# Transposing quantised FFN rows in float32r: DMA copies of thirteen batches into float32r tiles, with the remaining order of steps written anew

## The chip, the cores and the metric

The kernel runs on one core of a Trainium2 chip. The engines are named as in the profile: PE is the matrix engine (PEld its weight loads), DVE the vector engine, ACT the scalar engine, POOL the general engine, SP the engine that issues most DMAs. The metric is the time on the device of one execution, in microseconds, of which a smaller one is better. Times are given as the median of several runs; the profile is of one further execution.

## The reference

One transformer layer over `x` of 16 batches, 256 rows and 256 columns, in float32. What matters here is its last part, a gated FFN whose inputs and weights are quantised in blocks of 16 along the last axis:

```python
def fp4_quant_dequant(x):
    xb = x.reshape(shape[:-1] + (shape[-1] // BLOCK, BLOCK))
    scale = jnp.max(jnp.abs(xb), axis=-1, keepdims=True) / 6.0
    scale = jnp.maximum(scale, jnp.float32(1e-12))
    xn = xb / scale
    idx = jnp.searchsorted(_MID, jnp.abs(xn))
    q = _GRID[idx] * jnp.sign(xn) * scale
    return q.reshape(shape)
...
gate = fp4_linear(x, w_gate)
y = fp4_linear(x, w_up)
h = jax.nn.silu(gate) * y
return fp4_linear(h, w_down)
...
x = x + _L0_attn_ref(_L0_cond_ref(x, mask_SxS_bk1, cond_256, ...), ...)
x = x + _L0_ffn_ref(_L0_cond2_ref(x, cond_256, ...), ...)
```

`fp4_linear` quantises both operands and multiplies. The hidden size is 704. Ahead of the FFN stand an attention with 16 heads and a modulated norm, a recurrence over the rows (RWKV), and a spectral rotation by quaternions.

## The kernel before

The work of each batch is cut into stages, each a Python generator that yields after a few instructions. A stage and a batch make a name of two characters: `a` asks (loads x, projects q, k and v), `t` attends, `l` leaves the attention (output projection and norm), `m` mixes (the recurrence), `r` rotates and quantises the FFN's input, `h` and `i` make the hidden rows of the first and second 128 rows of the batch (`hidden`), `d` and `e` transpose them (`turn_h`), `f` multiplies by the down weights (`down`). The batch is a hex digit. `W` and `V` are the weights of the FFN, prepared once by `in_weights` and `out_weights`.

The order of all instructions is written out by hand in `ORDER` (L28), 1884 names; each occurrence runs its generator up to the next `yield`, and within the block at L1113 every engine executes its instructions in just that order. `BANKS` (L83) gives for each of 749 PSUM tiles, in order of allocation, which of the eight banks it takes. An engine that waits holds up everything behind it in its own queue, SP included: it issues the loads of x (L165), the spreads of q and k by way of DRAM (L704 and L708, one store and eight loads each) and the stores of the output (L1091, L1064), in the order of the steps.

The hidden rows go this way, for each batch and 128 rows, in two chunks of 384 and 320 columns: PE computes gate and up in PSUM (L1003); ACT takes the tanh (L1015); DVE forms the product (L1017, L1019); `quant_bank` quantises it with DVE (L554 to L557), ACT (L559), DVE again (L561, L562), and last POOL multiplies by the block scales into the SBUF tile `hq` (L564). `hq` has four buffers. `turn_h` (L1026) then has PE transpose the 704 columns of `hq` in six blocks of up to 128, three to a PSUM tile, in `turn_part` (L604, the transposes at L608), and ACT copies the result to `hT` (L1033 to L1037), from which `down` reads (L1072, L1079, and L1052 for the last batches). `turn_part` also serves the down weights in `out_weights`. `late(b)` (L662) is true for the last three batches, which take some other paths in `rotate` and `down`.

All of this is float32, and so are `ident` (L200), the identity matrix of the transposes, and `hq`. The one use of float32r, a type of four bytes for PE, is the attention's scores (L771), whose `qT` and `kT` tiles are of that type and are filled by DMA, with the source seen as float32.

Of the kernel before, what the change touches and what calls it, by code (L numbers as in the profile page):

```python
# [8 lines left out]
F32 = mybir.dt.float32  # L9
BF16 = mybir.dt.bfloat16  # L10
F32R = mybir.dt.float32r
# [7 lines left out]
P = 128  # L19
# [13 lines left out]
m0 m0 m0 a2 l1 a2 m0 l1 t2 W5 V0 R t2 t2 t2 a3 m0 V1 m0 m0 t2 t2 m0 W3 l1 t2 W3 m0 l1 m0 t2 t2 t2 t2 R t2 t2 t2  # L33
R m0 V0 t2 W0 W0 l1 m1 a3 W4 a3 a3 m0 V0 W3 l1 t2 m1 W3 a3 t2 t2 W2 W2 W0 A m1 m1 l2 A m1 m1 W4 l2 r0 m1 l2 m1
l2 r0 a4 a3 m1 m1 l2 l2 m1 m1 l2 m2 m1 m1 l2 m1 a3 m2 t3 a3 t3 m2 t3 t3 t3 m1 a4 t3 r0 r0 t3 r0 t3 a4 t3 t3 t3
m2 a4 t3 t3 a5 m2 W2 a4 V1 m2 t3 a4 t3 r0 t3 m2 m1 r0 t3 r0 a4 r1 m2 m2 a4 r1 t3 r1 r0 a4 W2 a5 a4 l3 l3 a6 m2
l3 V1 r1 m2 r0 a5 i0 a5 m2 i0 r1 r1 m2 i0 l3 V1 a4 t4 r1 m2 t4 t4 h0 i0 V1 t4 t4 i0 V1 m2 a5 t4 i0 h0 i0 h0 h0
t4 t4 i0 V1 t4 t4 t4 t4 i0 t4 a5 l3 t4 a5 r1 l3 r1 t4 m2 m2 h0 l3 a5 m3 l3 m3 t4 V1 a5 m3 i0 i0 a5 r2 r1 t4 h0
t4 m3 m3 r2 i0 m3 h0 a5 m3 l4 l4 a6 m3 l4 m3 m3 i0 a6 a5 l4 m3 m3 V1 a6 m3 t5 m3 t5 i1 i0 m3 t5 t5 i0 m3 t5 t5
e0 h0 i1 i1 e0 a6 t5 i1 t5 t5 t5 t5 h0 t5 t5 m3 i1 l4 t5 r2 a6 r2 t5 r2 l4 a7 t5 l4 i1 i1 d0 h0 i1 a6 h0 m4 r3  # L40
l4 m4 m4 h0 a6 a6 t5 d0 h1 m4 h0 r3 r2 i1 t5 h1 h1 a6 a6 i1 h1 m4 m4 h0 a7 r2 h1 i0 i1 h0 a6 h1 m4 a7 m4 a7 i1
m4 t6 h1 e0 t6 m4 m4 e0 t6 m4 l5 t6 i1 l5 t6 t6 r2 h0 d0 l5 m4 i1 h1 i1 t6 r2 m4 a7 m4 t6 d0 t6 l5 l5 t6 t6 r3
t6 t6 r3 t6 l5 a7 r2 e1 l5 r3 m4 a7 t6 d1 r3 i2 a7 r3 a7 f0 i1 i2 h2 i2 r3 i2 r3 f0 m5 l5 h2 e1 m4 a7 m5 a8 i2
h2 m5 h2 a7 i2 i2 h2 h1 r4 h2 h1 a7 h2 h1 d1 f0 h1 t7 i2 f0 t6 t7 f0 r4 t7 t7 h1 e1 t7 h1 m5 t7 t6 e1 t7 m5 h1
a8 t6 t7 m5 t7 t7 t7 a8 r4 h1 m5 t7 h2 d1 a8 r4 t7 d1 m5 r4 a8 a8 d2 l6 t7 m5 l6 l6 l6 i2 m5 i2 i2 r4 r3 m5 a8
i2 m5 r4 a8 l6 m5 h2 t7 a8 m5 h2 i2 h2 a8 m5 f1 l6 i2 m5 i2 i3 a9 a8 h2 h2 l6 i3 f0 f1 i3 h2 f1 i3 a8 l6 h2 m6
h2 d2 m6 m6 t8 f1 t8 t8 t7 t8 e2 i2 f1 i3 m5 t8 d2 r5 i3 i3 d2 r5 t7 a9 t7 t8 t8 t8 e2 t8 i3 e2 t8 a9 t8 a9 t8
t8 e3 m6 l7 m6 t8 l7 m6 t8 a9 r4 h3 h3 l7 l7 a9 r4 m6 m6 a9 l7 h3 e2 m6 a9 h3 l7 h3 a9 m6 m6 h3 f2 l7 i3 a9 i3
m6 i3 m6 h3 f2 i3 l7 m7 h3 m6 i3 i3 m6 m6 a9 aa m7 h3 i3 h3 h3 f1 h3 f2 m7 a9 e3 t9 t8 t9 t9 t9 f2 m6 r4 d3 f2
i3 t9 r6 h3 h3 t9 d3 e3 t8 h3 r6 t8 t9 h3 aa t9 t9 d3 e3 r5 r5 t9 r5 aa i4 i4 t9 l8 d3 t9 i4 m7 i4 aa i4 ab r5  # L50
h4 l8 i4 r5 m7 l8 h4 i4 f2 l8 aa t9 h4 h4 aa t9 m7 r5 h4 h4 l8 l8 i4 m7 h4 l8 t9 m7 m7 aa aa h4 m7 m7 i4 m7 m7
d4 m8 i4 i4 f3 aa aa l8 m7 m8 h4 m7 i4 i4 f3 m7 h4 m7 i4 m8 aa d4 r7 f3 h4 aa h4 i4 h4 ta f3 ta ta t9 f3 ta r7
ab h4 ac h4 ta e4 r7 t9 ab r7 e4 ta ab i4 ta r7 h4 r5 t9 ta ta r7 m8 ta ta ta ta r7 d4 r5 r6 ab r6 ta m8 m8 e4
m8 ab ab ta r6 m8 m8 m8 m8 l9 ab r6 h5 l9 m8 i5 h5 r6 i5 d4 m8 ab h5 l9 i5 h5 ab i5 e4 h5 i5 h5 h5 h5 ab l9 i5
m8 m8 r6 h5 h5 h5 tb h5 tb ta tb i5 tb m8 m8 r6 ab h5 l9 f4 tb l9 tb tb h5 i5 h5 tb e5 f4 ta ta e5 tb h5 tb tb
tb l9 f4 d5 r8 f4 f4 l9 tb r8 d5 r6 d5 ac m9 f4 tb r7 r8 r7 la tb la h6 h6 la r8 r8 h6 i5 i5 h6 m9 la d5 h6 la
i5 r7 i5 m9 m9 la ac m9 r8 m9 i5 m9 m9 ac i5 m9 la m9 ma m9 ac i6 m9 i7 m9 ac r8 h6 r8 ac m9 i5 i5 m9 i6 i6 ac
e5 m9 ac i7 h6 ac la i7 h6 ma e5 i6 f5 i7 f5 i6 i7 ma i6 i7 m9 f5 ad i6 f5 d6 h7 r9 h6 i6 i7 h6 h6 h6 ac f5 h7
h7 ac d6 tc tc r9 h6 tb h6 h7 tc ad tc ad ae h7 tc tc h6 tb h7 tc ad h7 tc tc tb r9 tc ad tc tc i7 ma h7 tc r9
h6 d6 ad i6 r9 ma tc e6 ma ad tc i6 i6 ma i6 h7 r9 r9 i7 f5 ma i6 r8 ma ad e6 r8 i6 lb ad h7 i7 h7 i6 h8 ma i6  # L60
i7 ma ad i7 ma e6 ma h7 h8 d6 i7 lb ad r9 e6 i7 h8 ma h7 ma r9 lb h7 i7 h8 td lb tc h7 ad td h8 td td td ma h8
lb h8 td e7 lb lb f6 lb f6 e7 mb td f6 i7 mb tc mb h8 ma tc h7 td td d7 f6 ra d7 i8 td f6 td i8 td ra r9 td e7
ae i8 i8 td d7 ra i8 mb i8 e7 f6 ra i8 i9 ae d7 i9 mb ra mb i9 i9 lc ra mb ae mb td h8 mb lc ae h8 i9 lc i8 i9
lc ra ae i9 lc mb h8 ae lc h8 mb h9 lc ra h8 mc ae h8 h9 h9 ra ae mb h9 ae h8 mb mb td d8 lc i8 h9 i8 mb h9 mc
mb f7 ra f7 h8 i8 mb i8 h9 f7 td d8 mc f7 te i8 f7 te rb rb ae te te td e8 i8 rb te te mc h9 i8 mc mc ae rb e8
af f3 rb ld ld rb i9 mc mc mc te ld rb mc te ld te mc mc te te ld mc te i8 te mc mc te mc te d8 af te e8 ld af
te e9 ld md h9 i9 h9 ld h9 te md md md af i9 af d8 mc af i9 md h9 md C rb i9 rb h9 af ha af md i9 e8 i9 md md h9
ha ha md ha f8 md ia ia ha af ia md md ia ha af h9 ia f8 md md i9 f8 ia ia af tf e9 rb tf f8 rc tf tf ia d9 tf
f8 ha tf ia md tf rc tf d9 tf rc i9 ha ia ia tf ia tf tf rc tf tf ia ea e9 e9 ib da rc tf h9 tf d9 ib ib f7 ia
ia le rc rc ib tf f8 le hb ib d9 hb rc tf hb ib le ha le hb le ha ib f9 rc le f9 md le hb ha hb da me ia ha le  # L70
hb ib ha f9 f9 ha ea ha rc ea me ea f9 eb me me me rd ha ib da hb ib me ib me db rd ib rd me rd lf me ib hb da
lf hb ib lf rd rd lf hb lf ib me rd me rd hb lf me hb me lf lf me rd rd ib fa fa hb me db mf eb hb eb hb fa me
db mf mf hc ic hc hc db me fa hc mf re ic fa ic hc ic re hc hc eb re mf ic re ic mf hc re re mf f9 fb re dc hc
fb hc re ic hc dc mf hc mf mf hc re mf mf hc ic ec hc fb mf ic ec ic hc hd ic mf dc mf re id ic ie mf hd ic dc
mf id fb id ic ic id ic hd rf hd id ec ec fc fb id ie rf rf ie id id fb rf fc hd rf ed id hd ed id id hd fc id
hd rf hd rf dd hd id rf ie dd hd he rf id hd he rf id id hd he ed hd he if ie ed hd hd ie if ie ie ie ie ie ie
dd dd he if if ie he he he fa fd ee he fd fd de ee if he ie he if he hf ie fd ie hf he if de he hf if ee he if
ee if ef if hf he hf de de hf fe if fe hf hf hf if hf hf if hf df hf if if fe ef hf hf C fc fe ff df ef ef hf fd
df df C fc fe C ff fc ff ff ff ff ff
"""  # L80


BANKS = """  # L83
0123456702 1345670521 3470521364 7320516473 0275164237 5164023571 6043175415 3752406175 2406137541 6035741604
3165042763 1504276315 0246701245 6012465307 2164375023 4756234571 0254371254 3172130671 2507136254 7163204617
3246172530 2615304527 0615627045 6207341502 6731502617 0341635042 3570143527 6013756021 3750425405 6130253607
4163075165 3210746251 0736251063 2416521425 7045273645 0273165407 3416523071 4530276135 2074630146 5370462715
3064537106 2536713460 2153470134 6702346753 6154321675 3421673245 7054763473 1052674273 1520731207 3561403256
1743256412 3054167401 5274301574 3065120373 4561207356 3074305126 4732065704 3215431275 0312670435 1274531604
7531045261 0675105402 5137205146 7250136247 5013473506 2435264053 7415602417 2516427460 3561207314 5017264210  # L90
7640327125 3020425264 6026516106 4106452410 156014205
"""


# [1 line left out]
def kernel(  # L96
# [28 lines left out]
    nc = tc.nc  # L125
# [4 lines left out]
    FF = w_gate.shape[0]  # L130
# [6 lines left out]
    const = ctx.enter_context(tc.tile_pool(name="const", bufs=1))  # L137
# [4 lines left out]
    wk = ctx.enter_context(tc.tile_pool(name="work", bufs=1))  # L142
# [5 lines left out]
    def bank(name):  # L148
        at = next(plan, None)
        if at is None:  # L150
            spare[0] = (spare[0] + 1) % 7
            at = 7 if name == "pss" else spare[0]
        return psum.tile([P, 512], F32, tag=f"bank{at}", name=name)

    def ps():
        return bank("ps")
# [42 lines left out]
    nc.scalar.activation(early, mhalf, AF.Exp)  # L199
    ident = const.tile([P, P], F32, tag="ident", name="ident")  # L200
    make_identity(nc, ident)


    blank = const.tile([P, P], F32, tag="blank", name="blank")
# [398 lines left out]

    def turn_part(src, k0):  # L604
        pt = ps()
        for k in range(k0, k0 + 3):
            n = min(P, FF - k * P)
            nc.tensor.transpose(pt[0:n, (k - k0) * P : (k - k0 + 1) * P], src[:, k * P : k * P + n], ident)  # L608
        return pt[:, 0 : 3 * P].rearrange("p (k t) -> p k t", t=P)

    def out_weights(t):
# [50 lines left out]
    late = lambda b: b >= B - 3  # L662

    xTs, qks, oTs, xns, ys, x1s, xqs, hqs = {}, {}, {}, {}, {}, {}, {}, {}
# [330 lines left out]
    def hidden(b, tt):  # L995
        xqT = xqs[b]
        hq = None
        for f0, n in ((0, 384), (384, FF - 384)):
# [20 lines left out]
            nc.vector.scalar_tensor_tensor(h[:, 0:n], th, 0.5, h[:, 0:n], ALU.mult, ALU.mult)  # L1019
            if f0 == 0:  # L1020
                hq = wk.tile([P, FF], F32, tag="hq", name="hq", bufs=4)
                hqs[b, tt] = hq
            yield from quant_bank(h, n, hq[:, f0 : f0 + n])


    def turn_h(b, tt):  # L1026
        hq = hqs.pop((b, tt))
# [234 lines left out]
```

## Time and profile before

| | |
|---|---|
| median of 3 runs | 645.34 us (645.21 to 646.45) |
| the profiled execution | 645.53 us, of which span 643.7 |
| granted PE clock | 1.000 |
| DMA | 57.72 MB, mean 90 GB/s |
| DVE L936, reciprocal of 128x512 | 16 x 3343 ns |
| ACT L781, exponentials of the scores | 256 x 609 ns |

The span is the time from the first to the last instruction; the rest of the execution's time lies around it. A row of the profile names a line and engine, what is written and read, the count, the busy time and the mean length of one, and the idle time before it with what ended it. For PE, busy time is the union of overlapping instructions: the mean length of a matmul is its latency, and the distance from start to start of two that follow each other is what it takes of the engine. A float32 matmul stands as two records, a transpose as one. Over the span in 40 slices, PE, DVE and the DMA engines are busy as follows, in tenths:

```profile
PE   9999999999999999999999999999999999999996
...
DVE  7897899889898877999998999999999999999994
...
DMA  6643525334251425333420334203204100001001
```

### The profile page before, as it was taken

The page shows a single profiled execution, that of the slowest core. Times are in us where ns is not written, and L with a number is a line of the kernel's source. Part 1 is how long each engine was busy: PE and PEld are TensorE (multiplying, and loading weights), DVE is VectorE, ACT ScalarE, POOL GpSimd, SP SyncE. Part 2 cuts the span into 40 slices and gives each one's busy share as a digit, 9 for nine tenths or more (in the row PEclk, how much of TensorE's full clock was granted, in tenths as well). Part 3 has the DMA queues.
Part 4 walks back from the last instruction along what each step waited for, and adds up shares of the span by engine and source line. Part 5 has one row for each costly group of instructions (what it writes and reads, how often), then busy time and mean ns, then how long its engine had stood idle before and what let it go on. Part 6 is the DMA issues. An engine that isn't in the chain of part 4 may idle for free.

```text
span 643.7 us, 11304 instructions
## 1 busy us (share of the span) xinstructions
PE 635.6 (99%) x3936; PEld 475.9 (74%) x3936; DVE 579.0 (90%) x1178; ACT 391.2 (61%) x903; POOL 161.4 (25%) x214
## 2 busy tenths in 40 slices
PE   9999999999999999999999999999999999999996
PEld 7568877677777778777777777777877778776675
DVE  7897899889898877999998999999999999999994
ACT  3879784776757577674766546666483755433332
POOL 3353213222231122131221313113130122112220
PEclk9999999999999999999999999999999999999999
DMA  6643525334251425333420334203204100001001
GB/s 169 172 149 120 167 87 174 99 99 133 82 166 35 154 57 166 78 100 116 148 67 18 126 102 149 67 17 131 82 34 151 47 2 16 1 1 35 0 26 46
DMA packets 62848, 57.72 MB, mean 90 GB/s; under 512 B 36912, under 2 KB 40896, under 8 KB 62784
## 3 DMA queue, kind: packets, MB, share of 16 engines
q1 hardware_dynamic: 62416, 56.65, 29.4%
q8 instruction: 33, 0.54, 0.4%
q10 hardware_dynamic: 368, 0.28, 0.1%
q14 instruction: 31, 0.25, 0.1%
HBM read 38.03 MB, written 18.87 MB: 88 GB/s over the span
## 4 chain that ended last, share of the span: by engine, by line
PE 83%; DVE 12%; issue 2%; ACT 1%; DVEq 0%; ACTq 0%
PE ps L632 24%; PE ps L1003 18%; PE ps L793 9%; PE ps L644 8%; PE ps L1072 7%; PE pss L771 5%; PE ps L608 3%; PE ps L965 2%; PE pss L763 2%; DVE v L562 1%; DVE ps L554 1%; PE ps L656 1%; DVE ps L561 1%; DVE ps L1019 1%; PE ps L1079 1%
## 5 line engine op out<-in xcount | busy, mean ns | idle before, releaser
L1003 PE MATMUL ps<-guT,xqT 128*128 128x320 f32 (+1 forms) x512 | 165.6, 461 | 0.6 <-DVE v L562 0.6
L781 ACT ACTIVATE w<-pss 128x512 f32<-128x512 f32 x256 | 133.6, 609 | 32.7 <-PE pss L771 28.8
L1003 PEld LDWEIGHTS ps<-guT,xqT 128*128 128x128 f32 x512 | 94.7, 190 | 42.0 <-DVE v L562 1.7
L564 POOL TENSOR_TENSOR hq<-v,am 128x320 f32<-128x320 f32 (+1 forms) x64 | 50.0, 787 | 175.8 <-DVE v L562 154.4
L698 POOL TENSOR_TENSOR two<-two 128x512 f32<-128x512 f32 x28 | 35.7, 1275 | 114.2 <-ACT two L691 79.1
L793 PE MATMUL ps<-w,v_one 128*32 128x256 f32 x1024 | 63.1, 382 | 0.1
L559 ACT ACTIVATE m<-ps 128x384 bf16<-128x384 f32 (+1 forms) x64 | 29.8, 467 | 53.2 <-DVE ps L557 52.9
L1072 PE MATMUL ps<-hT,downT 128*128 128x256 f32 x260 | 59.6, 379 | 0.0
L1072 PEld LDWEIGHTS ps<-hT,downT 128*128 128x128 f32 x260 | 48.8, 190 | 8.1 <-ACT w L781 0.3
L936 DVE RECIPROCAL den<-den 128x512 f32<-128x512 f32 x16 | 53.5, 3343 | 0.1
L793 PEld LDWEIGHTS ps<-w,v_one 128*32 128x32 f32 x1024 | 31.8, 109 | 25.3 <-ACT w L781 3.6
L1015 ACT ACTIVATE th<-ps 128x320 f32<-128x320 f32 (+1 forms) x64 | 29.8, 469 | 26.9 <-PE ps L1003 26.1
L771 PEld LDWEIGHTS pss<-qT,kT 64*128 64x128 f32 x448 | 31.0, 185 | 19.3 <-issue 8.9
L771 PE MATMUL pss<-qT,kT 64*128 64x256 f32 x448 | 42.6, 306 | 0.1
L561 DVE SCALAR_TENSOR_TENSOR ps<-m,ps 128x384 f32<-128x384 bf16 (+1 forms) x64 | 33.2, 518 | 6.0 <-ACT m L559 5.8
L562 DVE SCALAR_TENSOR_TENSOR v<-m,ps 128x384 f32<-128x384 bf16 (+1 forms) x64 | 33.3, 521 | 4.9
L557 DVE SCALAR_TENSOR_TENSOR ps<-ps,rs 128x320 f32<-128x320 f32 (+1 forms) x64 | 34.1, 533 | 2.2
L554 DVE TENSOR_REDUCE ps<-ps 128x20 f32<-128x320 f32 (+1 forms) x64 | 34.1, 532 | 2.2
L608 PE MATMUL ps<-ident,hq 128*128 128x128 f32 (+1 forms) x204 | 34.5, 283 | 0.4 <-POOL hq L564 0.2
L1019 DVE SCALAR_TENSOR_TENSOR ps<-th,ps 128x320 f32<-128x320 f32 (+1 forms) x64 | 33.2, 518 | 1.1 <-PE ps L1003 0.4
L1017 DVE SCALAR_TENSOR_TENSOR th<-th,ps 128x320 f32<-128x320 f32 (+1 forms) x64 | 32.1, 507 | 0.4 <-ACT th L1015 0.3
L608 PEld LDWEIGHTS ps<-ident,hq 128*128 128x128 f32 (+1 forms) x204 | 22.0, 136 | 13.1 <-issue 4.0
(200 smaller groups left out, 1288.2 us busy)
## 6 DMA issues: line engine op xcount, KB each, us to landing
kept<-two SPq DMA_DIRECT2D x28, 512.0 KB, 3.2
qT<-kept SPq DMA_DIRECT2D x112, 128.0 KB, 2.9
kT<-kept SPq DMA_DIRECT2D x112, 128.0 KB, 2.8
x_sb<-in_x_dram SPq DMA_DIRECT2D x64, 64.0 KB, 2.3
out_dram<-o_sb SPq DMA_DIRECT2D x52, 64.0 KB, 1.9
out_dram<-o_sb SPq DMA_DIRECT2D x6, 128.0 KB, 2.3
raw<-in_L_ffn_w_down_dram SPq DMA_DIRECT2D x2, 352.0 KB, 3.9
raw<-in_L_ffn_w_gate_dram SPq DMA_DIRECT2D x5, 128.0 KB, 3.3
```

Of the source, the lines that this page charges most:

```text
L554: nc.vector.tensor_reduce(top, blk(x), AX.X, ALU.max, apply_absolute_value=True)
L562: nc.vector.scalar_tensor_tensor(v, m, BASE, x, ALU.max, ALU.subtract)
L564: nc.gpsimd.tensor_tensor(blk(dst), blk(v), bc(am), ALU.mult)
L608: nc.tensor.transpose(pt[0:n, (k - k0) * P : (k - k0 + 1) * P], src[:, k * P : k * P + n], ident)
L632: nc.tensor.matmul(pool_tile[:, ot * n : (ot + 1) * n], w[:, ct, ot * P : (ot + 1) * P], src[ct], start=(ct == 0), stop=(ct == E2 - 1),)
L644: nc.tensor.matmul(pool_tile[:, tt * E : (tt + 1) * E], srcT[:, ct, tt * P : (tt + 1) * P], w[:, ct, :], start=(ct == 0), stop=(ct == E2 - 1),
L771: nc.tensor.matmul(quad[2 * s + r][:, i * S : (i + 1) * S], kT[rows_, 2 * r + i, g, ks], qT[rows_, 2 * r + i, g, :], start=True, stop=True,)
L781: nc.scalar.activation(w[kt][:, r].rearrange("p i q -> p (i q)"), quad[r], AF.Exp)
L793: nc.tensor.matmul(pu[32 * r : 32 * r + 32, i * S : (i + 1) * S], vo[:, kt, 8 * g + 2 * r + i, :], w[kt][:, r, i, :], start=(kt == 0), sto ...
L936: nc.vector.reciprocal(flat(den), flat(den))
L1003: nc.tensor.matmul(p_[:, 0:n], xqT[:, ct, tt * P : (tt + 1) * P], guT[:, ct, base : base + n], start=(ct == 0), stop=(ct == E2 - 1),)
L1072: nc.tensor.matmul(pdn[:, 0:S], downT[:, k, h * P : (h + 1) * P], hT[:, k, :], start=(k == 0), stop=False)
```

## The change

For the thirteen batches that are not `late`, each quantised chunk of the hidden rows is copied by a DMA on SP's queue from `hq` to a new tile `hr` of type float32r, with the destination seen as float32, and `turn_h` transposes `hr` in place of `hq`. `hr` has two buffers of 128 x 704. `turn_part` uses a new identity `ident_r` of that type and sees the PSUM tile as float32r when its source is; the ACT copies out of PSUM are as before. The last three batches and the down weights keep their float32 transposes. `hidden` yields twice more per row tile in those batches, so `ORDER` has 1936 names: its first 299 are the same, the rest are in a new order. `BANKS` has 749 places as before and is new from the tenth on.

```diff
-m2 a4 t3 t3 a5 m2 W2 a4 V1 m2 t3 a4 t3 r0 t3 m2 m1 r0 t3 r0 a4 r1 m2 m2 a4 r1 t3 r1 r0 a4 W2 a5 a4 l3 l3 a6 m2
+m2 a4 t3 t3 a5 m2 W2 a4 V1 m2 t3 a4 t3 r0 t3 m2 m1 r0 t3 r0 a4 a4 a4 r1 m2 r1 t3 m2 m2 l3 W2 a5 r0 m2 r1 a5 r1
...
-0123456702 1345670521 3470521364 7320516473 0275164237 5164023571 6043175415 3752406175 2406137541 6035741604
+0123456701 2345675012 3475012364 7135026471 5307264130 7265413074 2653470540 3701562470 1536427054 6320754635
...
     ident = const.tile([P, P], F32, tag="ident", name="ident")
     make_identity(nc, ident)
 
+    ident_r = const.tile([P, P], F32R, tag="ident_r", name="ident_r")
+    nc.scalar.copy(ident_r, ident)
+
...
     def turn_part(src, k0):
         pt = ps()
+        fast_ = src.dtype == F32R
         for k in range(k0, k0 + 3):
             n = min(P, FF - k * P)
-            nc.tensor.transpose(pt[0:n, (k - k0) * P : (k - k0 + 1) * P], src[:, k * P : k * P + n], ident)
+            dst = pt[0:n, (k - k0) * P : (k - k0 + 1) * P]
+            nc.tensor.transpose(
+                dst.bitcast(F32R) if fast_ else dst, src[:, k * P : k * P + n], ident_r if fast_ else ident
+            )
         return pt[:, 0 : 3 * P].rearrange("p (k t) -> p k t", t=P)
...
             if f0 == 0:
                 hq = wk.tile([P, FF], F32, tag="hq", name="hq", bufs=4)
-                hqs[b, tt] = hq
+                if not late(b):
+                    hr = wk.tile([P, FF], F32R, tag="hr", name="hr", bufs=2)
+                hqs[b, tt] = hq if late(b) else hr
             yield from quant_bank(h, n, hq[:, f0 : f0 + n])
-
+            if not late(b):
+                nc.sync.dma_start(out=hr[:, f0 : f0 + n].bitcast(F32), in_=hq[:, f0 : f0 + n])
+                yield
```

## The prediction

> **What bounds the kernel now.** I read the busy rows and the chain first, then windows of three stretches, then who made VectorE (DVE) wait in them. Busy and chain, from the page:
>
> ```profile
> PE 635.6 (99%) x3936; PEld 475.9 (74%) x3936; DVE 579.0 (90%) x1178; ACT 391.2 (61%) x903; POOL 161.4 (25%) x214
> ...
> PE 83%; DVE 12%; issue 2%; ACT 1%; DVEq 0%; ACTq 0%
> ```
>
> The chain is PE's up to about 559 us and DVE's from there to 632. That would make every saved matmul a gain, so I looked at the stretches (length, then PE, PEld, DVE, ACT, POOL busy):
>
> ```profile
> 85.00:360.00 275.00, 274.70 (x1792) 205.81 (x1791) 244.37 (x480) 182.84 (x415) 66.49 (x73) 1.00 0.34 103
> 360.00:559.00 199.00, 198.87 (x1187) 149.53 (x1186) 190.00 (x386) 113.52 (x268) 46.35 (x54) 1.00 0.25 75
> 559.00:632.60 73.60, 72.53 (x331) 53.46 (x330) 68.63 (x153) 27.84 (x72) 15.29 (x19) 1.00 0.05 14
> ```
>
> DVE is busy 89% of the first stretch, 95% of the second, 93% of the third. Its waits (total, times, longest), the largest before 360 us and all after it:
>
> ```profile
> DVE bs L898 <- ACT ps L907: 6.1, 1, 6.1
> DVE ps L561 <- ACT m L559: 5.5, 6, 2.4
> DVE ps L919 <- PE ps L632: 2.7, 2, 1.5
> ...
> DVE res L1085 <- PE ps L1079: 0.4, 1, 0.4
> DVE x1T L949 <- PE ps L632: 0.4, 1, 0.4
> DVE ps L561 <- ACT m L559: 0.2, 1, 0.2
> ```
>
> From 85 to 360 us its waits add up to 20.1 us, from 360 us to the end to 1.4 us; the rest of its idle time there is pauses under 0.1 us between its own instructions. So **two engines share the bound**: PE until about 360 us, and then PE and DVE together. Work taken from PE after 360 us shortens little, because DVE has no wait left that it could fill.
>
> **The transposes.** Thirteen batches of two row tiles of six blocks are 156 of L608's 204 transposes. Rows by form (busy, mean ns), and two timeline lines (start, length):
>
> ```profile
> L608 PE MATMUL ps<-ident,hq 128*128 128x128 f32 x170 | 31.1, 285 | 0.4 <-POOL hq L564 0.2
> L608 PEld LDWEIGHTS ps<-ident,hq 128*128 128x128 f32 x170 | 19.3, 140 | 13.1 <-issue 4.0 <-POOL hq L564 2.5 <-ACT mx L876 0.4
> L771 PE MATMUL pss<-qT,kT 64*128 64x256 f32 x448 | 42.6, 306 | 0.1
> L771 PEld LDWEIGHTS pss<-qT,kT 64*128 64x128 f32 x448 | 31.0, 185 | 19.3 <-issue 8.9 <-ACT w L781 3.4 <-DVE on L812 1.2
> ...
> 312.54 0.74 PE L771 MATMUL pss<-qT,kT 64*128 64x256 f32 x8
> ...
> 314.46 0.49 PE L608 MATMUL ps<-ident,hq 128*128 128x128 f32 x3
> ```
>
> The 285 ns is latency, not cost. Three f32 transposes take 0.49 us, and the last takes 0.273 from its start, so two steps are 0.217: **109 ns each**, 0.85 ns a column. The only float32r work is the scores (L771, shown as f32). Its eight matmuls are four pairs side by side; in the records' starts the pairs follow at 0.22, 0.12 and 0.12 us. The first step is a weight load that nothing hid; 118 ns for 256 columns is 0.46 ns a column, so 128 columns would be 59 ns. Weight loads could spoil that. L608's load takes 140 ns for 128 columns and 111 for 64 (the 64-row form), thus 58 per 128 plus a fixed part. L771's 185 against 109 for 32 columns (L793) is 101 per 128. A float32r transpose that loads as L608 does steps at 59, one that loads as L771 does at about 101, and one whose time is set by the instruction rather than its columns at L771's full 118, which is 9 ns dearer than today. No row shows it. I take 80, midway between 59 and 101, because operation and columns are L608's and only the type is L771's.
>
> Here a rule has to be weighed. The Trainium skill, "TensorE: Matmul & The Clock Gate", Part 4, puts a transpose at about 275 ns in a kernel, most of it the access to SBUF[...]. By the rule the sum is 0. The row agrees with 273 to 285 ns of latency, but the step of 109 shows that in a group it is pipelined away, so I go by the row. By the same page's Terms ("4× faster for FP32" of the transpose mode) the step should be a quarter of an f32 matmul's two records, 2 x 109 / 4 = 54 ns; today's 109 is only half, so there is room for a faster type.
>
> Sum on PE: after each group of three comes mostly an f32 matmul, whose load (190 ns, about 108 of it columns) starts only when the third transpose does. So the third still costs 109. Two of three, 104, save 29 ns: **3.0 us**; ends 104 x 50 = 5.2 (7.8 if all 156 gain) and 156 x -9 = -1.4.
>
> How much is felt: about 72 of the 156 (batches 0 to 5) stand before 360 us, where PE alone decides: 48 x 29 = 1.4 us. Of the other 1.6 I count half, as the new order may draw DVE's work forward. Together about 2.2 us.
>
> **The copies.** 52 DMAs, 192 KB and 160 KB by turns, 9.4 MB. Now 56.65 MB take 29.4% of the DMA engines; these add some 5%. On SP each holds the queue for 0.45 us (x_sb's issues) to 0.59 (qT's): 52 x 0.5 = 26 us. SP is in order: a spread of q or k (L704, L708) occupies it for 0.4 + 2.9 + 8 x 0.59 = 8 us, so a copy behind one waits, and behind a waiting copy stand spreads, loads of x and stores of out. Landing: 1.9 us (out, 64 KB), 2.3 (x), 2.9 (qT), 3.2 (kept, 512 KB); I take 2.6. I walked the new recorded order, adding PE's steps between each POOL multiply (0.8 us) and the first transpose that reads it, with SP's queue and the two hr buffers. Of the 52, 39 have 5 us or more between issue and use. With 2.6 us of landing three come late, by 2.2, 0.5 and 0.1 us; the 2.2 is the very last copy, of batch 12, in the stretch where DVE decides. I count 0.7 us of loss. The spreads do not suffer: their smallest margin after landing is 2.5 us, against 2.0 before.
>
> Two hr buffers: a copy waits for the transposes two row tiles earlier; in the walk that never comes last in a late case. hq's four buffers come free at the copy's landing, earlier than now.
>
> **The rest.** ident_r is one ACT copy, 0.3 us by L1037's 262 ns; ACT idles from 2.7 to 8.6 us (it waits for PE L632), which hides it; without that cover it would hold back qT L726 by 0.3. Sixteen more semaphore instructions on PE cost nothing while its queue runs ahead; 13 of today's ended 4.0 us of idle PEld, 0.3 each, so at worst 5 us.
>
> The new order starts to differ near 99 us. It has as many changes of line on PE (448 and 448), and DVE's work set before a given point of PE's agrees within 3 us throughout. Operands of PE are somewhat earlier (from ACT under 1.5 us ahead: 45 cases against 61 between 75 and 350 us of PE's work), those of DVE later (from ACT under 2.5 us: 128 against 109). For PE, L793 and L771 wait 3.6 and 3.4 us for ACT today; a quarter fewer tight cases of these 7.0, half of it felt, is a gain of 0.9. For DVE I book nothing. The bounds are 4 us either way: on one side about the largest single wait (6.1) less that gain, on the other a fifth of the 20.1.
>
> **Sum** against the profiled run (645.53: span 643.7 and 1.8 around it): -2.2 + 0.7 - 0.9 = -2.4, **643.1 us**; the median, 645.34, is 0.2 below the profiled run.
>
> **Rivals.**
> - *Hidden anyway.* DVE is the bound, its order is equally good, and PE's savings become waits: 645.3. For: 1.4 us of DVE waits after 360. Against: 20 us before.
> - *Slower: the copies arrive late at PE.* Place: the 13 copies with under 5 us from issue to use, six of them after 500 us, where neither engine has slack. Price: with 4 us of landing (out's longest is 3.8, qT's 4.4) the shortfalls add up to 3.6 + 1.9 + 1.5 + 1.2 + 0.5 + 0.3 = 9 us, 7 after what PE saves: 651. It decides from about 3.2 us, where the shortfalls (5) pass the saving. Against: 2.3 us is usual for such sizes.
> - *The type does not pay.* Steps at 109 to 118: +1.4, late copies 0.7 to 2: 647.5. That would be the change not doing what it says.
> - *The order leaves one more long wait on DVE*, like L898's 6.1 us: 649.
>
> **From this to the numbers.** No change is what this kernel's runs cannot tell, 0.2% or 1.3 us. Faster (638.5 to 644) 0.43; hidden 0.13; late copies 0.19; type 0.12; order 0.13. So faster 0.43, same 0.13, slower 0.44: the forecast is the likeliest single case though slower is as likely in sum. Range 638.5 to 650.5; the forecast's own range is 638.5 to 644.
>
> **What would show it.** Transposes of hr at steps of 59 to 85 ns, 109 where an f32 matmul follows; PE's busy time 2 to 6 us less; copies landing in 2 to 3 us; no wait of PE on hr over 2 us; DVE's waits between 85 and 360 us below 20. I am wrong if the steps stay at 109, if PE waits for DMAs of hr for over 3 us in all, or if DVE waits longer than before.

## The result, and the profile after

The kernel after takes **647.65 us** (646.66 to 647.99), the kernel before in the same comparison 645.44 us (645.21 to 646.45): a ratio of **1.0028**, 95% interval 1.0018 to 1.0039. It is 1.8 us slower; the forecast was 2.4 us faster. A second measurement gave 1.0028 again (1.0019 to 1.0036).

Most of the rows that the prediction watched do what it said; the steps of the transposes, shown below, do so only in part. The busy row and the chain of the page after, in the order engine, busy us, share of the span, instructions:

```profile
PE 633.3 (98%) x3936; PEld 472.3 (73%) x3936; DVE 580.6 (90%) x1178; ACT 392.2 (61%) x904; POOL 162.2 (25%) x214
...
PE 87%; DVE 7%; ACT 2%; issue 2%; DMA 1%; SPq 0%; POOL 0%; DVEq 0%; ACTq 0%
```

PE is busy 2.3 us less (635.6 before) and the chain leans more on it. The same three stretches as before (length, then PE, PEld, DVE, ACT and POOL busy, clock, DMA share):

```profile
85.00:360.00 275.00, 274.73 (x1795) 204.38 (x1794) 247.59 (x484) 180.39 (x411) 68.36 (x75) 1.00 0.39 121
360.00:559.00 199.00, 198.97 (x1193) 149.16 (x1192) 188.94 (x383) 117.69 (x276) 45.48 (x53) 1.00 0.29 92
559.00:632.00 73.00, 70.27 (x322) 51.73 (x321) 68.61 (x153) 26.88 (x69) 15.32 (x19) 1.00 0.10 28
```

Up to 360 us DVE gets 3.2 us more done than before (244.37), because its waits there fell from 20.1 to 16.6 us. From 360 to 559 us, where it has no slack, it is busy 1.1 us *less* than before (190.00) in the same time. After 559 us PE is busy 1.7 us less than before in the same stretch, as I cut it here (71.93 before, by the same cut to 632.00). So the lead is built up early and lost late. Two views show where it ends. The waits of PE between 85 and 640 us (total, times, longest), the largest:

```profile
PE ps L614 <- DMA hr<-hq: 1.6, 1, 1.6
PE ps L1011 <- DVE v L566: 0.6, 1, 0.6
PE ps L515 <- ACT hT L1049: 0.4, 1, 0.4
```

One wait of 1.6 us, at 587 us, is put down to the last copy. And the end of the timeline (start, length, instruction), first before, then after:

```profile
637.67 2.54 SPq L1064 DMA_DIRECT2D out_dram<-o_sb  x2
...
638.90 0.38 ACT L1061 COPY o_sb<-ps 128x256 f32<-128x256 f32 x1 [2.65 <-PE ps L1052]
```

```profile
637.03 2.43 SPq L1103 DMA_DIRECT2D out_dram<-o_sb  x2
...
638.25 0.38 ACT L1073 COPY o_sb<-ps 128x256 f32<-128x256 f32 x1 [2.65 <-PE ps L1064]
639.57 0.40 SPq L1076 DMA_DIRECT2D out_dram<-o_sb  x1
```

The last computation, ACT's copy into `o_sb`, ends at 638.63 us, 0.65 us **earlier** than before (639.28). But the span ends at 645.7, 7.0 us later; before, 4.4 us lay between. In this pair of profiles the whole loss is behind the last compute instruction. In the kernel before the last store was issued 0.55 us after the copy, SP had the signal of its landing 3.0 us later, and 0.95 us after that all was over. In the kernel after these three parts are 0.94, 3.8 and 2.3 us. A second profile of the kernel after (646.98 us) splits its loss otherwise: the copy ends at 639.57, 0.3 us later than before, and the end comes 5.6 us behind it. So about 1.2 us of the tail is in both profiles, the rest in one.

The transposes themselves, by form (duration of one: minimum, median, maximum, in ns; the records call float32r f32):

```profile
L614 PE MATMUL ps<-ident_r,hr x156: 221/250/520, 123.2 to 588.0; 128*128 128x128 f32 x130, 128*64 128x128 f32 x26
...
L614 PE MATMUL ps<-ident,hq x48: 272/273/329, 43.6 to 633.0; 128*128 128x128 f32 x40, 128*64 128x128 f32 x8
```

From start to start, the three steps of a group (to the second, to the third, to what follows) have medians of 116, 86 and mostly 60 to 86 ns in the 52 groups, the last of them by what follows; with the type undone (below) they are 164, 109 and 109. Part of that is paid back by the float32 matmul behind a group: it now starts while its own weights are still being loaded, and its step to the next matmul grows by some 60 ns (in 25 groups from 218 to some 282, in 16 from 325 to 384).

### The profile page after: what moved, and what is told of

It reads as the page before. It is cut to its first block, busy times and chain, and to the rows that moved or that the text cites. A ratio compares the mean times of both kernels' runs of the same rounds, so it can differ in the third digit from the quotient of the medians.

```text
span 645.7 us, 11442 instructions
## 1 busy us (share of the span) xinstructions
PE 633.3 (98%) x3936; PEld 472.3 (73%) x3936; DVE 580.6 (90%) x1178; ACT 392.2 (61%) x904; POOL 162.2 (25%) x214
## 4 chain that ended last, share of the span: by engine, by line
PE 87%; DVE 7%; ACT 2%; issue 2%; DMA 1%; SPq 0%; POOL 0%; DVEq 0%; ACTq 0%
PE ps L640 24%; PE ps L1011 20%; PE ps L801 9%; PE ps L652 8%; PE ps L1084 7%; PE pss L779 5%; PE ps L614 3%; PE ps L1064 2%; PE ps L973 2%; PE pss L771 2%; PE ps L664 1%; PE ps L1091 1%; DVE v L566 1%; DVE ps L558 1%; DVE ps L1027 1%
## 5 line engine op out<-in xcount | busy, mean ns | idle before, releaser
L563 ACT ACTIVATE m<-ps 128x320 bf16<-128x320 f32 (+1 forms) x64 | 29.8, 465 | 49.0 <-DVE ps L561 48.7
L566 DVE SCALAR_TENSOR_TENSOR v<-m,ps 128x320 f32<-128x320 bf16 (+1 forms) x64 | 33.4, 521 | 4.5
L947 POOL TENSOR_TENSOR yT<-num,den 128x512 f32<-128x512 f32 x16 | 20.4, 1276 | 64.3 <-DVE den L944 52.2
L565 DVE SCALAR_TENSOR_TENSOR ps<-m,ps 128x320 f32<-128x320 bf16 (+1 forms) x64 | 33.1, 517 | 0.5 <-ACT m L563 0.3
L640 PE MATMUL ps<-yT,wt_ao 128*128 128x256 f32 x128 | 30.8, 383 | 0.2 <-POOL yT L947 0.2
```

The source lines that it names most:

```text
L566: nc.vector.scalar_tensor_tensor(v, m, BASE, x, ALU.max, ALU.subtract)
L640: nc.tensor.matmul(pool_tile[:, ot * n : (ot + 1) * n], w[:, ct, ot * P : (ot + 1) * P], src[ct], start=(ct == 0), stop=(ct == E2 - 1),)
```

## Experiments: what lies behind the last compute instruction

The first theory was that the tail is the loss, and that it has two causes: the slow path, which this input never enters, now issues its copies from SP and not POOL, which leaves SP eight more semaphore instructions at the branch (L1222) that it steps through; and the order of the last stores. The rivals were the order inside, late copies, and the type.

**The slow path's queue.** The kernel after, with

```diff
-                nc.sync.dma_start(out=hr[:, f0 : f0 + n].bitcast(F32), in_=hq[:, f0 : f0 + n])
+                queue[0].dma_start(out=hr[:, f0 : f0 + n].bitcast(F32), in_=hq[:, f0 : f0 + n])
```

`queue[0]` is SP on the fast path and POOL on the slow one, so nothing on the fast path changes.

> The kernel after, except that in the slow path, which this input never enters, the copies are issued by POOL as that path's other DMAs are; the fast path keeps every instruction. If the loss lies behind the last compute instruction, where SP steps through 8 semaphore instructions of the branch not taken after the last store has landed: the 8 are gone, the end comes about 1 us sooner after the last landing, and the time is 646.0 to 646.8 against 647.65 of the change; less if the last store then also lands sooner (645.3). If the loss lies in the new order, in late copies or in the type: 647.2 to 648.0, unchanged.

Measured: 646.99 us, ratio 1.0001 (0.9991 to 1.0011). On this chip the kernel before scattered between 645.3 and 648.3 us, so I ran the kernel after again beside variants of itself, on one chip:

> The kernel after, unchanged, a second time, beside variants of itself. If the loss is the kernel's own: a ratio to before of 1.0018 to 1.0039 again. If the equal time of the variant with POOL issuing the copies in the slow path came from the chip it ran on: about 1.000.

Measured: 647.56 us, 1.0028 (1.0019 to 1.0036). A further variant, on the same chip, was meant to move a step of the stores as well:

> The variant whose slow path issues its copies from POOL, with one step moved in the last line of the order: batch 12's four stores are issued before, not after, the first store of the last batch; no compute instruction moves. If the stores of batch 12 hold SP ahead of the last store, and put its packets in front of PE's instruction fetch that comes 2.6 us after PE's last matmul: the last store is issued within 0.6 us of the last compute instruction (1.0 now), lands 2.5 us after that (3.9 now), and the time falls by 1.0 to 1.9 us, ratio to before 0.997 to 0.9986. If the late landing has nothing to do with the order of the stores: ratio 0.999 to 1.001, as without the move.

Measured: 646.24 us, 1.0007 (1.0001 to 1.0014). The step stood where SP's queue keeps the order of the stores all the same, so the edit did nothing to them (SP's timeline shows one store of the last batch, batch 12's four, then the last, as before it). It serves as a repeat of the variant above: on one chip, 647.56 falls to 646.24 when the eight semaphore instructions go, **1.3 us**, give or take 0.7. The waits of SP after 634 us, in the kernel after and in the variant:

```profile
SPq L1076 <- ACT o_sb L1073: 4.2, 1, 4.2
SPq L1222 <- SPq L1222: 1.9, 2, 1.7
SPq L1270 <- PEq L1270: 0.7, 2, 0.5
```

```profile
SPq L1076 <- ACT o_sb L1073: 4.2, 1, 4.2
SPq L1270 <- DMA out_dram<-o_sb: 1.6, 1, 1.6
SPq L1270 <- PEq L1270: 0.7, 2, 0.5
```

In the kernel after SP waits for the last landing at the branch, L1222, until 643.35 us (the view names SP itself; the landing's own signal stands at 643.34); only then come the other semaphore instructions of the branch, 0.07 us each, and the twelve at L1270, 643.69 to 644.76. In the variant SP waits for the landing among those twelve. Work that could have been done beside the landing is done behind it. The same in the kernel before, which shows the cost alone:

```diff
-            queue[0].dma_start(
+            nc.sync.dma_start(
                 out=out[b].rearrange("(q i) (a c) -> a i q c", i=32, a=4)[a], in_=o_sb[32 * a : 32 * a + 32]
```

> The kernel before, except that in the slow path, never entered, the result's stores are issued by SP instead of POOL; the fast path keeps every instruction. If semaphore instructions of the branch not taken delay the end: SP has more of them at the branch, the distance from the last store's landing to the end grows by 0.5 to 1.2 us, and the time is 646.0 to 646.6 against 645.44. If they cost nothing: 645.2 to 645.7.

Measured: ratio 1.0013 (1.0003 to 1.0023), 0.8 us; this was on the chip where the kernel before scatters by 3 us. Code that is never run costs 0.8 to 1.3 us here.

**The order of the last stores.** The new order puts batch 12's four stores between the last batch's two; the old one has them ahead of both. The step (`fc`) moved ahead, in the variant, and behind, in the kernel before; on the other engines no instruction moves:

```diff
-... df C df C ff ff ff ff fe fc ff ff
+... df C df C fc ff ff ff ff fe ff ff
```

> The variant whose slow path issues its copies from POOL (ratio 1.0001 and, run again, 1.0007), with batch 12's four stores now really ahead of the last batch's first store on SP's queue; the other four engines keep every instruction in place. If the order of the six last stores makes the last one late: the last store is issued about 0.5 us after the last compute instruction instead of 1.0, lands 2.5 us after its issue instead of 3.6 to 4.1, and the end comes 4.3 to 4.8 us after the last compute instruction instead of 5.6 to 6.3: ratio 0.9975 to 0.9990. If the landing depends on PE's instruction fetch alone, which comes 2.6 us after PE's last matmul whatever SP does: 1.0000 to 1.0010.

```diff
-df df C fc fe C ff fc ff ff ff ff ff
+df df C fc fe C ff ff ff ff fc ff ff
```

> The mirror of it: the kernel before, with batch 12's four stores moved between the last batch's two stores, as the kernel after has them; only SP's queue changes. If the order of the stores costs: the distance from the last compute instruction to the end grows from 4.4 to between 5.6 and 6.3 us, ratio 1.0015 to 1.0030. If not: 0.9995 to 1.0005.

Measured: 0.9995 (0.9984 to 1.0006) where the variant had 1.0001 and 1.0007; and 1.0020 (1.0011 to 1.0029) in the kernel before. The end of SP's timeline in the variant with the stores ahead, and in the old kernel with them behind:

```profile
635.17 1.82 SPq L1103 DMA_DIRECT2D out_dram<-o_sb  x4
637.12 2.70 SPq L1076 DMA_DIRECT2D out_dram<-o_sb  x2
```

```profile
637.06 3.50 SPq L1091 DMA_DIRECT2D out_dram<-o_sb  x4
640.65 0.79 SPq L1064 DMA_DIRECT2D out_dram<-o_sb  x1
```

With the stores ahead the last one is issued 0.7 us after ACT's copy and the end comes 4.5 us after that copy; with them behind, 1.0 and 6.2. So the order of six stores costs the old kernel **1.3 us**, though in the forward direction only about 0.6 of it shows, in a comparison of ratios from different chips, and the ratio forecast for it, 0.9975 to 0.9990, was missed. Nor is it a fixed price: in the profile of the order alone (below) the stores stand behind too, and the end comes only 4.4 us after the copy. Why the last store mostly lands later is seen in the DMA records as a coincidence, told at the end.

## Experiments: the type, the copies and the order

The tail accounts for most of the loss, but not for where 2.4 us of gain went. For this I count from an instruction that all kernels share, a DVE instruction near 61 us ahead of the place where the orders part, to the end of PE's last matmul; 577.84 us in the profile of before, 577.28 in that of after. This distance leaves out the start and the tail. Two more profiles in the old order and in float32 (the slow path's queue, the stores behind) have 578.11 and 578.04.

**The type undone**, order and copies kept:

```diff
-                    hr = wk.tile([P, FF], F32R, tag="hr", name="hr", bufs=2)
+                    hr = wk.tile([P, FF], F32, tag="hr", name="hr", bufs=2)
```

> The kernel after, its copies and its order kept, but the copied rows stay float32 and are transposed in float32. If the float32r transposes save PE about 50 ns in each group of three (52 groups, 2.6 us): PE's busy time 635.5 to 636.2 against 633.3, and the time 1 to 2.6 us longer than the change's, 648.6 to 650.3. If the type pays nothing, or DVE hides it: 647.2 to 648.2.

Measured: ratio 1.0055 (1.0041 to 1.0070). Its busy row:

```profile
PE 636.3 (98%) x3936; PEld 475.4 (73%) x3936; DVE 581.9 (90%) x1178; ACT 392.4 (60%) x904; POOL 162.2 (25%) x214
```

PE is busy 3.0 us more than in the kernel after, and the distance is 579.96: **the type saves 2.7 us**, all but 0.3 of what it takes off PE. On the same chip the variant with POOL in the slow path took 646.99 us and this one 651.02; the 4.0 us between them are what the type's 2.7 and the branch's 1.3 would make.

**The type alone**, in the old order. No copies; POOL writes the rows straight into float32r, with `ident_r` and `turn_part` as in the kernel after:

```diff
-                hq = wk.tile([P, FF], F32, tag="hq", name="hq", bufs=4)
+                hq = wk.tile([P, FF], F32R, tag="hq", name="hq", bufs=4)
```

> The kernel before, its order kept and no DMA copies; POOL writes the quantised rows straight into float32r tiles, which rounds them to that type (this part of the computation differs), and all 16 batches are transposed in float32r. If the type pays in itself: PE's busy time falls by 64 groups at 50 ns, 3.2 us, to about 632.4, and the time to 642.3 to 644.5. If PE's savings become waits for DVE: 645.0 to 645.7. If the type does not pay: 645.4 or more.

> The type alone, in the old order, a second time: rows written straight into float32r tiles (rounded), all 16 batches transposed in that type. If the saving of PE is felt in full: the last compute instruction ends 2 us earlier from the same early DVE instruction, ratio 0.9958 to 0.9972. If the first run's ratio came from the scatter of the kernel before on that chip, and only part is felt: 0.9975 to 0.999.

Measured: 0.9958 (0.9944 to 0.9972) and 0.9972 (0.9960 to 0.9983), 644.39 us both times; PE's busy time in the first is 632.6, and the distances are 575.91 and 576.47, 1.4 to 1.9 us below before. On these two chips the kernel before took 647.02 and 646.50 us, more than in the first comparison, so the ratios may flatter; the distances are the steadier measure. This kernel beats both.

**The copies taken away**, order kept (the second of these carries the same ineffective move of a step as above, so it is the first again):

```diff
-                hq = wk.tile([P, FF], F32, tag="hq", name="hq", bufs=4)
-                if not late(b):
-                    hr = wk.tile([P, FF], F32R, tag="hr", name="hr", bufs=2)
-                hqs[b, tt] = hq if late(b) else hr
+                hq = wk.tile([P, FF], F32 if late(b) else F32R, tag="hq", name="hq", bufs=6)
+                hqs[b, tt] = hq
...
-                nc.sync.dma_start(out=hr[:, f0 : f0 + n].bitcast(F32), in_=hq[:, f0 : f0 + n])
```

> The order of the kernel after, with no copies: POOL writes the quantised rows of the thirteen batches straight into float32r tiles (which rounds them; this part of the computation differs), with six buffers where four and two were. If the copies cost time in themselves (PE's wait of 2 us for the last one, SP's queue held): the last compute instruction ends 1 to 2 us earlier than with them (637 to 638 us against 638.6 to 639), ratio to before 0.997 to 0.9987. If what eats the savings is the new order: no change by more than 0.4 us in the last compute instruction's end, ratio 0.9992 to 1.001.

> Both edits of the two kernels before this one: no copies, and batch 12's stores ahead of the last batch's first. If each of the two theories holds they add: 2 to 3.5 us below before, ratio 0.9945 to 0.997, as good as the old order with rows written in float32r (0.9958). If the new order loses: 0.998 or more.

Measured: 1.0004 (0.9996 to 1.0012) and 1.0003 (0.9994 to 1.0011): what the variant with copies has. And PE's wait at 587 us is still there, the same length, with another name. The waits of PE after 500 us in the second of them:

```profile
PE ps L614 <- DVE x1T L957: 1.6, 1, 1.6
PE ps L1011 <- DVE v L566: 0.6, 1, 0.6
```

The group of transposes needs a PSUM bank that DVE's addition into `x1T` (L957) has to give back. In the kernel after the copy's landing was signalled at 587.66 us, 0.06 us behind DVE's addition (587.60), and the view named the one that came last. Two releasers stood behind one wait; taking the copy away left 1.56 of its 1.62 us.

**The order alone**: no copies and float32 rows, nothing new that runs but the sequence of steps, two more buffers of `hq` and the copy into an unused `ident_r`. Against the variant with the copies taken away:

```diff
-                hq = wk.tile([P, FF], F32 if late(b) else F32R, tag="hq", name="hq", bufs=6)
+                hq = wk.tile([P, FF], F32, tag="hq", name="hq", bufs=6)
```

> The new order alone: float32 rows and float32 transposes as in the kernel before, no copies (six buffers in the place of four and two), and no new instructions at the branch not taken. If the new order is what loses: the last compute instruction ends about 2 us later than before's when both are counted from the same early DVE instruction, the end comes 1.2 to 1.8 us further behind it because of the order of the last stores, and the ratio to before is 1.0035 to 1.0055. If the order is neutral or gains, as the prediction had it, and the copies or the type lose: 0.9985 to 1.001.

Measured: ratio **1.0051** (1.0035 to 1.0067), 3.3 us. The distance is 579.95: the order costs **2.1 us** of computing time, and with the copies (579.96, the type undone) it costs the same, so the copies cost nothing that shows. Between the same two instructions PE stands idle for 3.4 us, against 2.0 before: 1.4 of the 2.1 us are waiting, which the one wait at L614 makes up, and in the other 0.7 PE is busy longer, for which no cause was found. The profile does not bear out the rest of the forecast, a longer way to the end: from the last compute instruction to the end it has 4.4 us, as before, and instead it began 1.5 us late (its first loads land later: PE waits 0.8 us for `ek` up to 4.74 us). The largest wait of PE after 500 us, and the three stretches:

```profile
PE ps L614 <- DVE x1T L957: 1.6, 1, 1.6
```

```profile
85.00:360.00 275.00, 274.70 (x1791) 205.31 (x1790) 246.64 (x478) 180.31 (x410) 67.65 (x74) 1.00 0.34 105
360.00:559.00 199.00, 198.97 (x1184) 148.62 (x1183) 188.22 (x379) 118.17 (x277) 44.89 (x53) 1.00 0.23 71
559.00:632.00 73.00, 70.32 (x315) 51.83 (x314) 68.43 (x151) 26.57 (x69) 15.22 (x18) 1.00 0.06 15
```

DVE is 1.8 us less busy between 360 and 559 us than in the kernel before (190.00), and PE 1.6 us less busy after 559: DVE falls behind first, then PE waits for it at the step that stands at 587 us in the kernel after (here at 592, the late start included). If every DVE instruction still to come is valued at its usual distance to the next in the trace of before, and the time counted from the shared early instruction, this order has some 0.6 us less DVE work left at 360 us than the old one, and 2.5 to 3 us more at 559 us. Two things in DVE's records of this stretch go with that. Pauses of 0.1 us or more add up to 5.0 us in 34 places, against 3.3 us in 27. And a DVE instruction that does not read what the one ahead of it wrote starts some 82 ns before that one's end, one that does read it 34 ns after: such early starts are 181 here and 192 before. An early start lost thus costs some 0.12 us.

**Less work for DVE**, in the variant with the new order, type and copies:

```diff
-            nc.vector.scalar_tensor_tensor(th, th, 1.0, gate, ALU.add, ALU.mult)
+            if b not in (11, 12):
+                nc.vector.scalar_tensor_tensor(th, th, 1.0, gate, ALU.add, ALU.mult)
```

> The variant whose slow path issues its copies from POOL, without the eight DVE multiplications of (tanh + 1) by the gate in batches 11 and 12, some 4 us of DVE's work between about 500 and 590 us (this part of the computation is left out). If DVE, late after 360 us in this order, is what takes back PE's savings: PE's wait of 1.6 us at 587 us is gone, the last compute instruction ends 1.5 to 2.5 us earlier, ratio 0.9965 to 0.9985. If the wait there is for the copy's landing, or PE alone decides: the wait stays and the ratio is 0.9995 or more.

Measured: 0.9981 (0.9972 to 0.9990), about 1.5 us below the variant; the distance is 575.59, 1.7 below. The waits of PE after 500 us:

```profile
PE ps L1011 <- DVE v L566: 0.6, 1, 0.6
PE ps L614 <- DMA hr<-hq: 0.5, 1, 0.5
```

Of the 1.6 us, 0.5 are left. The view names the copy again, but its landing (586.83 us) is again only 0.06 us behind DVE's addition into `x1T` (586.77), and the copy itself could be issued only after DVE and POOL had made its data. So DVE is what took back the saving here; what the copy would cost by itself cannot be told from this wait.

**One more attempt at the tail**, a miss. The type alone, with the very last store issued by ACT right behind its own copy:

> The kernel before with rows written straight into float32r (ratio 0.9958), and the very last store issued by ACT, right behind the ACT copy that makes its data, instead of by SP. If SP's queue holds that store back: it is issued 0.1 us instead of 0.55 us after the copy and the end comes 0.3 to 0.9 us sooner, ratio 0.9945 to 0.9954. If the end is set otherwise: 0.9955 to 0.9962.

Measured: 0.9989 (0.9981 to 0.9998), not better than 0.9958 and 0.9972 with SP, though these are ratios from three chips (in time 644.83 us against 644.39 twice). The store was issued 0.04 us after the copy instead of 0.56 to 0.58, yet the end came 4.9 us after the copy against 4.3 and 4.1. Its packets had ended at 640.03, but SP then waited 1.4 us for a semaphore instruction of ACT at the branch (L1218), until 642.0. An earlier issue alone does not bring the end forward.

## Why the prediction was wrong, step by step

The sum was -2.4 us. As the runs have it:

| step | predicted | measured |
|---|---|---|
| type, on PE | -3.0 | -3.0 (PE's busy time, type undone) |
| type, felt | -2.2 | -2.7 |
| copies | +0.7 | 0.0 (579.96 against 579.95) |
| new order, computing | -0.9 | **+2.1** (order alone) |
| order of the last stores | not in the sum | **+0.6 to 1.3** (+1.3 in before, stores behind) |
| semaphores of the branch | not in the sum | **+0.8 to 1.3** |
| together | -2.4 | +0.8 to +2.0; the comparison says +1.8 |

- **What bounds the kernel** was read rightly: PE to about 360 us, then both. The chain moving to PE, the early DVE waits falling from 20.1 to 16.6 us and the DVE work left out in batches 11 and 12 (a gain of 1.5 us for 4 us of DVE) all bear it out. One reading was off: DVE's pauses after 360 us are not all under 0.1 us; from 360 to 559 us 27 of 0.1 us or more add up to 3.3. But I drew half of it only: I asked what PE's savings are worth where DVE has no slack, and not what the new order does to DVE there.
- **The transposes.** The assumed step of 80 ns, with the third at 109 for the load behind it, gave 3.0 us, and that is PE's saving, in part by luck. The 109 ns of the first step was read from one group; of the 73 groups of the kernel before, 38 have over 150 there and 30 under 120. The largest gain is there (164 to 116), the second step is near the assumed size (86), and the third is short too (60 to 86): a group gains some 100 ns, not 58, and the matmul behind it gives some 60 back. The Trainium skill's "TensorE: Matmul & The Clock Gate", Part 4, gives its 275 ns for a bf16 transpose and compares no types; taking a sum of 0 from it was a conclusion of mine. In these traces a duration of that size is the latency, 250 ns now and 273 before; the choice of the row over the rule was right. My estimate of 54 ns from the 4x in the same page's Terms, which do not say what it is measured against, is neared only by the shortest steps, 59 to 64.
- **How much is felt**: 2.7 of 3.0, not 2.2. In this order PE, not DVE, carries most of the chain.
- **The copies.** They land in 2.5 us (192 KB) and 2.1 (160 KB), about as assumed, and the one foreseen to be late by 2.2 us is the one that the view names for PE's wait of 1.6 us. It still cost next to nothing: DVE gave back the bank at the same moment. SP's queue, held some 0.5 us by each of 52 issues, cost nothing either.
- **The new order is the step that failed.** "For DVE I book nothing", and 0.9 of gain for PE. What I counted was how early operands are ready by instruction counts, and that DVE's work ahead of a given point of PE's "agrees within 3 us throughout". In the stretch where DVE has 1.4 us of waits to spare, 3 us is no agreement; it is more than the forecast gain. What the runs show in its place is a cost of 2.1 us in computing. I had given 4 us either way as the bound of this term (by the wait that I named for it, 6.1 less 0.9, it would have been 5.2 on the slow side), and then let it enter the forecast with the other sign.
- **The tail** is the second step that failed. The sum took "span 643.7 and 1.8 around it" as fixed and so put at nothing, without a reason, what the runs show as 1.4 to 2.6 us. The last six stores stand in the order that I had before me, and the copy's fixed queue stands in the diff beside a slow path whose other DMAs go by `queue[0]`. I counted SP's queue only up to the last copy.
- **The rivals.** The slower side was given 0.44, most of it to late copies (651) and a long DVE wait (649). Late copies did not happen (651 for them takes off the order's 0.9 as well as the type's gain). The order rival has the right culprit, but not in one long wait of DVE's: it is lost in many small pauses and neighbours, and in a wait of PE for DVE. None of the three signs that I named as proof of being wrong came true, and the forecast was wrong all the same: none of them looked at DVE's pace after 360 us or behind the last compute instruction.

What stays open: which swaps in the order cost DVE its early starts and pauses; no single one was tried. That these put DVE behind is read from the records alone; that DVE's being behind costs PE time is shown by the run that leaves DVE work out. The shares of the tail are measured to about 0.6 us only, since one kernel's runs differ by 2 to 3 us on some chips. Two profiles of the new order with float32r rows, among them the kernel after run again, have a distance of 578.2, 0.9 us longer than the five others, with a DVE wait of 0.8 us more after 559 us; against these two the type saves 1.8 us, not 2.7, and the 0.0 of the copies is no finer than that.

## What to carry to other kernels

When an order is rewritten together with a faster operation, sum up for each engine that can be the bound how much work it has left at a few points of time, and take differences of a few microseconds there as seriously as the saving itself. A wait in the profile has one name but may have two causes: before paying for the named one, ask what else arrives at that moment. And look behind the last compute instruction: which store is issued last, what stands ahead of it in its queue, and what semaphores an unused branch leaves on the engine that has to wait for it.

## What the runs showed of the hardware, unexpected

- A branch that is not taken leaves SP with eight semaphore instructions when DMAs in it are issued by SP: about 0.07 us each, and they hold back what follows if one of them waits for the last landing (1.7 us here, until 643.35).
- An execution has 33 DMA packets of 16 KB of instructions, mostly 12 to 30 us apart; I take them to be PE's, which has the most instructions, but no record says so. The last ones take 1.0 to 1.9 us, and one comes 2.2 to 3.4 us after PE's last matmul in the profiles of all these kernels. In the kernel before it started at 641.46 us and the last store's packets ended at 642.32; in the kernel after it started at 640.73, only 1.2 us after the issue of the last store, and the packets ended at 642.88, with none ending between 641.5 and 642.2. Where the last store was issued 1.7 us before the fetch (stores ahead) they ended at 641.55. In all 16 profiles it goes by this distance: where the fetch starts 1.1 to 1.3 us after the issue of the last store (eight profiles), its packets end 3.2 to 3.8 us after the issue; where it starts 1.6 us or more after (eight), they end after 1.9 to 2.5. Two of the second kind, the kernel after run again and the order alone, have the stores behind like most of the first. So the order of the stores seems to act by putting the issue up to 0.5 us later, closer to the fetch. That the fetch delays the store is inferred from these times, and no run moved the fetch by itself. In most of these profiles one of SP's issues just before the end took 1.5 to 2.2 us instead of 0.45, during the fetch before that one.
- In these records DVE overlaps neighbours that do not depend on each other by some 82 ns and leaves 34 ns between those that do. An order of steps may thus be worth something to DVE even where nothing waits.
